# Constants behind the graph's building on ScalarE's queue, x on SyncE's queue, and a fourth buffer for early rows

## The chip, the cores and the metric

The kernel runs on one core of a Trainium2 chip. A core has a matrix engine (TensorE, "PE" in the profile), three engines for other arithmetic (VectorE "DVE", ScalarE "ACT", GpSimd "POOL"), a synchronising engine that mostly starts transfers (SyncE, "SP"), and 16 DMA engines that move data between HBM and the on-chip memory. Any of ScalarE, GpSimd and SyncE can start a transfer from its own queue; a queue is worked off in order. The metric is the device time of one launch in microseconds; smaller is better.

## The reference

One layer of a graph network over 3125 nodes with 256 features. `x` is normalised, sent nine times through the sparse adjacency given by 53,125 weighted edges (the first product is shared by all heads, so that the kernel needs three), mixed by a linear attention, and then sent through a gated network of eight experts.

```python
xn = _layernorm(x, axis=-1)
x = x + _L0_gnn_ref(xn, W0, b0, W1, b1, edge_weight, src, dst) + _L0_mix_ref(xn[None], ...)[0]
x = x + _L0_ffn_ref(_layernorm(x, axis=-1)[None], gate_w, gate_b, w1, b1, w2, b2)[0]

def _L0_gnn_ref(inputs_emb, W0, b0, W1, b1, edge_val, edge_row, edge_col):
    h = _spmm(edge_row, edge_col, edge_val, inputs_emb)
    for _ in range(HEADS):
        outputs = h
        for l, (W, b) in enumerate([(W0, b0), (W1, b1)]):
            z = _spmm(edge_row, edge_col, edge_val, outputs)
            AxW = jax.nn.softmax(z @ W.T + b, axis=1)
            outputs = AxW if l == 0 else jnp.concatenate([AxW, AxW], axis=1)
            ...
```

`dst` is sorted, so the edges of a node lie in one run.

## The kernel before

**Stages.** `from_runs` (L425) first builds a dense adjacency of 3200 x 3200 numbers in HBM (`adj`), from the runs of edges. Then the adjacency, in seven strips of up to 512 columns (`STRIPS`), is multiplied with `xn`, with the result `h` and with the first layer's output: three sweeps over seven strips, each strip 25 rows of 128 x 512. Key/value attention, the gate and the experts are interleaved with and follow these sweeps.

**The building.** It has an order written out by hand (`tc.manual_schedule`), so each engine runs its instructions in the order of the program text.
- `search(c)` (L479) finds, with one matmul (L482) and a few small VectorE operations (L485 to L491), where the runs of 125 groups of five nodes begin. There are five searches; three stand ahead of the first batch and two in the loop, after batches 4 and 6.
- `gather(c)` (L504) issues three indirect transfers on GpSimd's queue: sources, targets, weights (L510). `turn_ends` and `turn_some` bring them into place (transposes L539, ScalarE's copies L542).
- `load_x` (L365) asks for x in two pieces of 12 and 13 tiles of 128 nodes (`X_PIECES`), each behind one of the first two gathers, on GpSimd's queue. The second piece has a tail of 53 rows with a transfer of its own (L113).
- The loop over 40 batches (L698) handles 16 groups at a time: `prepare` makes one-hot operands (VectorE, L615, `selections` L588, `lhs` L624), `widen` casts one of them (ScalarE, L637), `batch` (L643) runs 16 groups of matmuls (L652), copies the sums out in four pieces (ScalarE, L656, `st_rows`), and SyncE writes the batch to `adj` in two transfers (L665 for 112 partitions, L666 for 13).
- As rows of `adj` are finished, `ask` has SyncE load them again (`load_rows`, L668 to L672): tag `a0` for the first strip with four buffers, tag `a1` for the second strip with three. `take` multiplies a loaded row into its strip's sum (L273). In the last batches three `a1` rows are asked for (L733); behind the loop the rest of strip 0 and 15 rows (`AHEAD`) of strip 1 follow. The last row of a strip has 53 nodes.
- `norm_a` to `norm_d` normalise x strip by strip inside the loop.

**The constants.** `make_constants` (L278) reserves memory for the weights of the graph layers, the gate's weights and bias, four normalisation rows and some index tables, in a pool that is open from the start to the end. It returns ten transfers for GpSimd's queue, which are issued behind the third gather (L686), and a generator that forms two gate constants by a matmul with `ones` at batches 22 and 23. `load_w_kv` (L418) is called at batch 24, on GpSimd's queue; w_q, w_o and b_o (L807 to L809) follow behind the building, the gate's rows (in `spread_gate`) much later, all on the same queue.

**Behind the building.** `total` and `found` (L744 to L749) check with one matmul that all edges were met; `found` lies in the pool `build`. Then `ph.close()` gives the building's memory back, and `load_part` (L250) loads blocks of five rows (`at`, L259, with L264 for a strip's 53-row tail) into five buffers in memory that was the building's.

**Semaphores.** The tile framework gives each transfer started by SyncE or ScalarE one of eight completion semaphores, in turn, and lets a transfer wait until the earlier user of its semaphore has landed. GpSimd's transfers have eight of their own.

Of the kernel before, what the change touches and what calls it, by code (L numbers as in the profile page):

```python
# [16 lines left out]
P = 128  # L17
N = 3125
D = 256
# [55 lines left out]
def gps_layer(ctx: ExitStack, tc: tile.TileContext, a: dict, out: bass.AP):  # L75
# [201 lines left out]

    def make_constants():  # L278
        loads = []

        def load(dst, of):
            loads.append(lambda: nc.gpsimd.dma_start(dst, of))

        w0T = const.tile([P, 2, HD], FP)
        load(w0T, a["w0T"].rearrange("(c p) n -> p c n", p=P))
        w1T = const.tile([P, HD], FP)
        load(w1T, a["w1T"])
        b0 = const.tile([P, 1], FP)
        load(b0, a["b0"].rearrange("(p one) -> p one", one=1))
        b1 = const.tile([P, HD], FP)  # L290
        load(b1, rows_all(a["b1"], 0, HD))
# [6 lines left out]
        ones = const.tile([P, P], FP)  # L298
        nc.vector.memset(ones, 1.0)
# [26 lines left out]
        key_base = const.tile([1, NEXP], FP)  # L326
        nc.vector.tensor_copy(key_base, ki)
        held.update(
            w0T=w0T, w1T=w1T, b0=b0, b1=b1, gate_b=gate_b, gate_c=gate_c, gate_m=gate_m, g_lo=g_lo, ones=ones, upto=upto,
            rev=rev, qi=qi, run=run, tok=tok, s_idx=s_idx, key_base=key_base, ln=ln,  # L330
        )

        def finish():

            pm = mm()
            for d in range(2):
                nc.tensor.matmul(
                    pm[:, :NEXP], ones, gate_w[:, d, :], start=(d == 0), stop=(d == 1)
                )
            yield  # L340
            nc.vector.tensor_scalar(gate_m, pm[:, :NEXP], 1.0 / D, None, op0=ALU.mult)
            nc.vector.tensor_tensor(
                gate_c, gate_w, gate_m[:, None, :].to_broadcast([P, 2, NEXP]), ALU.subtract
            )

        return loads, finish()

# [9 lines left out]
    def layer(net, runs):  # L357
# [60 lines left out]
        def load_w_kv():  # L418
            nc.gpsimd.dma_start(w_kv, a["wkv"].rearrange("(c p) n -> p c n", p=P))

# [4 lines left out]
        def from_runs():  # L425
# [13 lines left out]
            for queue, p0, p1, n in (  # L439
# [4 lines left out]
                ))  # L444
            loads, finish = make_constants()
            fi = find.tile([P, 1], I32)
# [32 lines left out]
            def search(c):  # L479
# [6 lines left out]
                    lt, p[:GC, :EK], g_thr[:GC, one],  # L486
                    held["ones"][:GC, 0:1].to_broadcast([GC, EK]), op0=ALU.is_lt,
                    op1=ALU.mult, accum_out=start[:, one],
# [12 lines left out]
            edge_h = build.tile([P, 2, NG + NG % 2], BF)  # L501
            matched = build.tile([GC, NC], FP)

# [52 lines left out]
            fetched = []  # L556
            for c, piece in enumerate(X_PIECES):
                search(c)
                fetched.append(gather(c))
                load_x(nc.gpsimd, *piece)  # L560
            search(2)
            turn_ends(0, *fetched[0])
            turn_some(0, fetched[0][0], edge_h, 1, 2)
# [121 lines left out]
            fetched.append(gather(2))  # L685
            for load in loads:  # L686
                load()

# [9 lines left out]
            for b in range(last + 1):  # L698
# [45 lines left out]
            total = mm()  # L744
            nc.tensor.matmul(total[:1, :NC], held["ones"][:GC, 0:1], matched, start=True, stop=True)
            found = build.tile([1, 1], FP)
            nc.vector.tensor_reduce(found, total[:1, :NC], AX.X, ALU.add)
# [9 lines left out]
        else:  # L757
            general()
            load_w_kv()
            load_x(nc.scalar, 0, NT)  # L760
            for s in range(len(STRIPS)):
# [20 lines left out]
        if runs:  # L782
            to_hT(0, sums[0])


        w0T, w1T, b0, b1, gate_b, gate_c, gate_m, g_lo, ones = (
            held[x]
            for x in ("w0T", "w1T", "b0", "b1", "gate_b", "gate_c", "gate_m", "g_lo", "ones")
        )
# [913 lines left out]
```

## Time and profile before

| | us |
|---|---|
| median of 3 runs | 1017.81 (1017.23 to 1018.5) |
| the profiled execution | 1018.58 |
| its span | 1016.6 |
| TensorE waits in 40 to 290, all releasers | 10.4 |
| the loop's last matmul group starts | 214.37 |
| ScalarE's last copy of `st_rows` starts | 214.79 |
| 60 matmuls on the last 15 rows, start | 224.52 |
| the check of the edge count on TensorE (L745), start | 250.66 |
| first load of an `at` block (L259), issue | 251.39 |

A row of a timeline reads: start, duration, engine, line, operation, output <- inputs, count, and in brackets the idle time ahead of it with what ended it. "PE acc L273 <- DMA a<-adj: 2.6, 2, 1.7" means that matmuls of L273 waited 2.6 us in all, twice, at most 1.7 us, for transfers from `adj` into `a0` or `a1` buffers (the profile leaves the digits out). In the list of transfers "to landing" is the time from the issue to the arrival of the data.

### The profile page before, as it was taken

What the parts mean: (1) busy time and instruction counts of PE and PEld (TensorE: products, weight loads), DVE (VectorE), ACT (ScalarE), POOL (GpSimd) and SP (SyncE); (2) the same over time, 40 slices, a digit from 0 to 9 for tenths busy, and PEclk for the clock granted to TensorE, in tenths of its full rate; (3) what the DMA queues carried; (4) which work ended last, traced back from release to release, by engine and by line L of the source; (5) the groups of instructions that cost most, each with busy time, mean ns of one, the idle gap of its engine ahead of it and who ended that gap; (6) DMA issues with size and microseconds to landing.
All of it is one profiled execution on the core that took longest, in us unless ns stands there. A gap on an engine that the chain in (4) does not pass through costs nothing.

```text
span 1016.6 us, 11457 instructions
## 1 busy us (share of the span) xinstructions
PE 980.6 (96%) x4202; PEld 639.6 (63%) x4202; DVE 514.3 (51%) x1149; ACT 304.6 (30%) x567; POOL 95.6 (9%) x113
## 2 busy tenths in 40 slices
PE   5899999989999999999999999999999989999996
PEld 3878888854444444455765554464544568888985
DVE  7999799800343444445653675584444454221211
ACT  3889889830000001001101001110111214224431
POOL 6411000000000000000000000000111132111111
PEclk9999999999999999999999999999999999999998
DMA  4989888983933247321475657769889896713310
GB/s 144 244 236 260 240 240 238 254 257 108 337 121 103 98 146 205 127 81 47 138 246 194 226 197 269 222 198 376 309 298 298 253 303 226 229 39 124 101 35 20
DMA packets 171641, 197.94 MB, mean 195 GB/s; under 512 B 7664, under 2 KB 118304, under 8 KB 171575
## 3 DMA queue, kind: packets, MB, share of 16 engines
q1 hardware_dynamic: 164285, 178.56, 56.3%
q0 software_dynamic: 7248, 18.51, 6.2%
q8 instruction: 35, 0.57, 0.2%
q14 instruction: 31, 0.25, 0.1%
q10 hardware_dynamic: 42, 0.05, 0.0%
HBM read 144.43 MB, written 53.37 MB: 195 GB/s over the span
## 4 chain that ended last, share of the span: by engine, by line
PE 85%; DMA 4%; DVE 4%; ACT 3%; issue 2%; SPq 1%; POOL 0%; POOLq 0%; ACTq 0%; DVEq 0%
PE acc L273 48%; PE mm L1203 7%; PE acc L1160 7%; PE acc L652 6%; PE b L652 5%; PE mm L831 4%; PE mm L887 2%; DMA at<-adj 2%; PE pk L859 1%; ACT rhs L637 1%; DMA adj<-st_rows 1%; ACT st_rows L656 1%; PE mm L914 1%; PE mm L1011 1%; PE mm L1150 0%
## 5 line engine op out<-in xcount | busy, mean ns | idle before, releaser
L273 PE MATMUL acc<-at,xn 128*128 128x512 f32 (+3 forms) x540 | 203.2, 523 | 1.5 <-DMA at<-adj 1.5
L273 PEld LDWEIGHTS acc<-at,xn 128*128 128x128 f32 (+1 forms) x540 | 96.5, 190 | 89.5 <-issue 75.1
L273 PE MATMUL acc<-at,late 128*128 128x512 f32 (+4 forms) x350 | 139.3, 549 | 3.9 <-DMA at<-adj 3.9
L273 PE MATMUL acc<-at,g 128*128 128x512 f32 (+4 forms) x350 | 137.8, 541 | 0.0
L273 PEld LDWEIGHTS acc<-at,late 128*128 128x128 f32 (+1 forms) x350 | 64.1, 195 | 63.7 <-issue 54.3
L273 PEld LDWEIGHTS acc<-at,g 128*128 128x128 f32 (+1 forms) x350 | 62.9, 190 | 58.6 <-issue 52.3
L652 PE MATMUL acc<-rhs,lhs 128*125 128x128 f32 x626 | 86.4, 282 | 9.0 <-ACT rhs L637 8.1
L652 PEld LDWEIGHTS acc<-rhs,lhs 128*125 128x125 f32 x626 | 78.3, 193 | 20.2 <-ACT rhs L637 9.3
L624 DVE TENSOR_TENSOR lhs<-in_row,in_blk 128x1000 f32<-128x1000 f32 (+1 forms) x79 | 90.3, 1185 | 1.2
L652 PE MATMUL b<-rhs,lhs 128*125 128x128 f32 x624 | 82.9, 277 | 0.0
L652 PEld LDWEIGHTS b<-rhs,lhs 128*125 128x125 f32 x624 | 76.4, 192 | 0.0
L273 PE MATMUL acc<-a,xn 128*128 128x512 f32 (+1 forms) x160 | 72.9, 594 | 2.6 <-DMA a<-adj 2.6
L637 ACT CAST rhs<-cells 128x2048 f32<-128x2048 bf16 x39 | 74.9, 1921 | 0.1
L844 ACT ACTIVATE sq<-kv 128x512 f32<-128x512 f32 x25 | 15.7, 629 | 179.4 <-DVE kv L840 179.4
L1203 PE MATMUL mm<-w,hm 128*128 128x256 f32 (+2 forms) x288 | 64.3, 380 | 0.0
L837 DVE TENSOR_REDUCE kmean<-mm 128x8 f32<-128x512 f32 x25 | 17.3, 691 | 91.6 <-PE mm L831 91.6
L1160 PE MATMUL acc<-xeT,w 128*128 128x208 f32 (+2 forms) x288 | 58.7, 361 | 0.7 <-ACT xeT L1154 0.7
L1203 PEld LDWEIGHTS mm<-w,hm 128*128 128x128 f32 (+2 forms) x288 | 51.2, 180 | 9.6
L1160 PEld LDWEIGHTS acc<-xeT,w 128*128 128x128 f32 x288 | 53.1, 190 | 4.4 <-ACT xeT L1154 0.9
L656 ACT COPY st_rows<-acc 125x512 f32<-125x512 f32 (+1 forms) x79 | 47.7, 603 | 25.2 <-issue 12.4
L1164 ACT ACTIVATE hm<-acc,b_e 128x256 f32<-128x256 f32 (+2 forms) x72 | 32.7, 454 | 65.5 <-PE acc L1160 65.5
L615 DVE TENSOR_TENSOR cells<-steps_w,edge_h 128x2048 bf16<-128x2048 bf16 (+1 forms) x40 | 47.7, 1193 | 4.5 <-ACT rhs L637 4.4
(271 smaller groups left out, 1035.3 us busy)
## 6 DMA issues: line engine op xcount, KB each, us to landing
at<-adj SPq DMA_DIRECT2D x52, 1280.0 KB
adj<-st_rows SPq DMA_DIRECT2D x39, 896.0 KB
at<-adj SPq DMA_DIRECT2D x14, 1024.0 KB
at<-adj SPq DMA_DIRECT2D x12, 960.0 KB
w<-in_f_w SPq DMA_DIRECT2D x10, 1024.0 KB
a<-adj SPq DMA_DIRECT2D x39, 256.0 KB
at<-adj SPq DMA_DIRECT2D x12, 452.5 KB
adj<-st_rows SPq DMA_DIRECT2D x39, 104.0 KB
```

What stands on the lines that cost most here:

```text
L273: nc.tensor.matmul(ps[d][:, :w], stationary(c, d)[:k], a_rows[:k, :w], start=(c == 0), stop=(c == NT - 1),)
L615: nc.vector.tensor_tensor(cells[:, :m, :, :k], steps_w[:, None, :, :k].to_broadcast([P, m, P, k]), of_pairs(1, g0, ng, P), ALU.is_equal,)
L624: nc.vector.tensor_tensor(lhs[:, j::k], in_row[:, j::k, :, None].to_broadcast([P, m, GR, CA]), in_blk[:, :, None, :, j].to_broadcast([P, m ...
L637: nc.scalar.copy(rhs.rearrange("p (i j) c -> p i j c", j=2), cells.rearrange("p i c j -> p i j c"),)
L652: nc.tensor.matmul(p[:GP, j * P : (j + 1) * P], lhs[:, j0 + j], rhs[:, j0 + j], start=True, stop=True,)
L656: nc.scalar.copy(st[:GP, j0 : j0 + nj, :], p[:GP, : nj * P].rearrange("p (g b) -> p g b", b=P),)
L831: nc.tensor.matmul(pkv, xnT[:, d, t * P : (t + 1) * P], w_kv[:, d, :], start=(d == 0), stop=(d == 1),)
L837: nc.vector.tensor_reduce(mean, p3, AX.X, ALU.add)
L887: nc.tensor.matmul(p[:, j * D : (j + 1) * D], xnT[:, d, (t0 + j) * P : (t0 + j + 1) * P], w_mix[:, d, :], start=(d == 0), stop=(d == 1),)
L1160: nc.tensor.matmul(p[:, :slots], w1[:, d, f * P : (f + 1) * P], xeT[:, d, :slots], start=(d == 0), stop=(d == 1),)
L1164: nc.scalar.activation(hm[:, f, :slots], p[:, :slots], AF.Relu, bias=b1_e[:, f : f + 1], scale=1.0)
L1203: nc.tensor.matmul(p[:n, :D], hm[:, f, c : c + n], w2[:, f, :], start=(f == 0), stop=(f == FC - 1),)
```

## The change

- `ones` is made at the start by itself. All other constants, with their index tables, go to a new pool `const_2` that is opened behind the building, in its memory. Their ten loads and that of `w_kv` are issued by ScalarE's queue, kept in the order of the program; w_q, w_o, b_o and the gate's rows are on ScalarE's queue as well. The gate's two constants are formed right there, behind the check of the edge count.
- x is asked for by SyncE's queue behind the third search; a one-element VectorE write into each piece's memory stands ahead of each request.
- Strip 1's early rows have four buffers, and the first of them is asked for one batch earlier, so that four come within the loop.
- `matched` and `found` lie in a pool that outlives the building.

In the built program the ten constant loads stand on ScalarE's queue directly behind its last copy of `st_rows`; on SyncE's queue the loads of strip 1's `at` blocks stand between the last loads of single rows.

```diff
+    ones = const.tile([P, P], FP)
+    nc.vector.memset(ones, 1.0)
+
+    def make_constants(const):
...
         def load(dst, of):
-            loads.append(lambda: nc.gpsimd.dma_start(dst, of))
+            tc.keep_in_program_order(nc.scalar.dma_start(dst, of))
...
-        def finish():
-
-            pm = mm()
-            for d in range(2):
-                nc.tensor.matmul(
-                    pm[:, :NEXP], ones, gate_w[:, d, :], start=(d == 0), stop=(d == 1)
-                )
-            yield
...
-        return loads, finish()
+        pm = mm()
+        for d in range(2):
+            nc.tensor.matmul(pm[:, :NEXP], ones, gate_w[:, d, :], start=(d == 0), stop=(d == 1))
+        nc.vector.tensor_scalar(gate_m, pm[:, :NEXP], 1.0 / D, None, op0=ALU.mult)
+        nc.vector.tensor_tensor(
+            gate_c, gate_w, gate_m[:, None, :].to_broadcast([P, 2, NEXP]), ALU.subtract
+        )
...
         def load_w_kv():
-            nc.gpsimd.dma_start(w_kv, a["wkv"].rearrange("(c p) n -> p c n", p=P))
+            tc.keep_in_program_order(
+                nc.scalar.dma_start(w_kv, a["wkv"].rearrange("(c p) n -> p c n", p=P))
+            )
...
-            loads, finish = make_constants()
...
-            matched = build.tile([GC, NC], FP)
+            matched = keep.tile([GC, NC], FP, tag="matched", name="matched")
...
-            for c, piece in enumerate(X_PIECES):
+            for c in range(2):
                 search(c)
                 fetched.append(gather(c))
-                load_x(nc.gpsimd, *piece)
             search(2)
+            for t0, t1 in X_PIECES:
+
+                nc.vector.memset(xa[:1, t0, :1], 0.0)
+                load_x(nc.sync, t0, t1)
...
-                at = first_a.tile([P, SW], FP, tag=tag, name=tag, bufs=4 if tag == "a0" else 3)
+                at = first_a.tile([P, SW], FP, tag=tag, name=tag, bufs=4)
...
-            for load in loads:
-                load()
...
-                if b in (22, 23):
-                    next(finish, None)
-                if b == 24:
-                    load_w_kv()
...
-                if last - 5 < b <= last - 2:
+                if last - 6 < b <= last - 2:
                     ask(more, ready_1, "a1")
...
-            found = build.tile([1, 1], FP)
+            found = keep.tile([1, 1], FP, tag="sum", name="found")
...
+        make_constants(net.enter_context(tc.tile_pool(name="const_2", bufs=1)))
+        load_w_kv()
...
-        nc.gpsimd.dma_start(w_q, a["wq"].rearrange("(c p) n -> p c n", p=P))
-        nc.gpsimd.dma_start(w_o, a["woT"].rearrange("(c p) n -> p c n", p=P))
-        nc.gpsimd.dma_start(b_o, rows_all(a["bo"], 0, D))
+        nc.scalar.dma_start(w_q, a["wq"].rearrange("(c p) n -> p c n", p=P))
+        nc.scalar.dma_start(w_o, a["woT"].rearrange("(c p) n -> p c n", p=P))
+        nc.scalar.dma_start(b_o, rows_all(a["bo"], 0, D))
...
-            nc.gpsimd.dma_start(raw, rows_all(a["gate_w"], 0, HD * NEXP).rearrange(
+            nc.scalar.dma_start(raw, rows_all(a["gate_w"], 0, HD * NEXP).rearrange(
```

More of the change, by code (lines that the diff above doesn't have):

```diff
@@ L276, in multiply @@
             )
-    def make_constants():
-        loads = []
+    ones = const.tile([P, P], FP)
+    nc.vector.memset(ones, 1.0)
+    def make_constants(const):
         def load(dst, of):
-            loads.append(lambda: nc.gpsimd.dma_start(dst, of))
+            tc.keep_in_program_order(nc.scalar.dma_start(dst, of))
         w0T = const.tile([P, 2, HD], FP)
@@ L295, in make_constants @@
         load(gate_b, rows_all(a["gate_b"], 0, NEXP))
-        ones = const.tile([P, P], FP)
-        nc.vector.memset(ones, 1.0)
         ln = const.tile([P, 4, 64], FP)
@@ L328, in make_constants @@
         held.update(
-            w0T=w0T, w1T=w1T, b0=b0, b1=b1, gate_b=gate_b, gate_c=gate_c, gate_m=gate_m, g_lo=g_lo, ones=ones, upto=upto,
+            w0T=w0T, w1T=w1T, b0=b0, b1=b1, gate_b=gate_b, gate_c=gate_c, gate_m=gate_m, g_lo=g_lo, upto=upto,
             rev=rev, qi=qi, run=run, tok=tok, s_idx=s_idx, key_base=key_base, ln=ln,
         )
-        def finish():
-            pm = mm()
-            for d in range(2):
-                nc.tensor.matmul(
-                    pm[:, :NEXP], ones, gate_w[:, d, :], start=(d == 0), stop=(d == 1)
-                )
-            yield
[L341 to L344, printed above, removed]
-        return loads, finish()
+        pm = mm()
[5 more added lines that the diff above has]
+        )
     y_end = keep.tile([P, 2, D], FP, tag="y_end", name="y_end")
@@ L486, in search @@
                     lt, p[:GC, :EK], g_thr[:GC, one],
-                    held["ones"][:GC, 0:1].to_broadcast([GC, EK]), op0=ALU.is_lt,
+                    ones[:GC, 0:1].to_broadcast([GC, EK]), op0=ALU.is_lt,
                     op1=ALU.mult, accum_out=start[:, one],
@@ L744, in from_runs @@
             total = mm()
-            nc.tensor.matmul(total[:1, :NC], held["ones"][:GC, 0:1], matched, start=True, stop=True)
-            found = build.tile([1, 1], FP)
+            nc.tensor.matmul(total[:1, :NC], ones[:GC, 0:1], matched, start=True, stop=True)
+            found = keep.tile([1, 1], FP, tag="sum", name="found")
             nc.vector.tensor_reduce(found, total[:1, :NC], AX.X, ALU.add)
@@ L758, in layer @@
             general()
-            load_w_kv()
             load_x(nc.scalar, 0, NT)
@@ L783, in layer @@
             to_hT(0, sums[0])
-        w0T, w1T, b0, b1, gate_b, gate_c, gate_m, g_lo, ones = (
+        w0T, w1T, b0, b1, gate_b, gate_c, gate_m, g_lo = (
             held[x]
-            for x in ("w0T", "w1T", "b0", "b1", "gate_b", "gate_c", "gate_m", "g_lo", "ones")
+            for x in ("w0T", "w1T", "b0", "b1", "gate_b", "gate_c", "gate_m", "g_lo")
         )
```

## The prediction

> **What bounds the kernel now.** The page's head comes first: the busy times, and the chain that ended last.
>
> ```profile
> PE 980.6 (96%) x4202; PEld 639.6 (63%) x4202; DVE 514.3 (51%) x1149; ACT 304.6 (30%) x567; POOL 95.6 (9%) x113
> ...
> PE 85%; DMA 4%; DVE 4%; ACT 3%; issue 2%; SPq 1%; POOL 0%; POOLq 0%; ACTq 0%; DVEq 0%
> ```
>
> TensorE is the bound: 36 us of 1016.6 are not its own, so an edit off TensorE gains only where TensorE stands idle, and loses wherever it opens new idle time. Next the stages by windows (columns: stretch and length, then busy time and count of PE, weight loads, DVE, ACT, POOL; granted clock; DMA share; GB/s).
>
> ```profile
> 18.60:43.10 24.50, 21.82 (x164) 20.86 (x164) 23.60 (x37) 18.46 (x25) 13.44 (x16) 1.00 0.97 246
> 43.10:62.50 19.40, 17.12 (x131) 16.24 (x132) 18.15 (x32) 18.67 (x27) 3.81 (x3) 0.91 0.98 272
> 62.50:95.00 32.50, 32.50 (x235) 27.15 (x234) 30.99 (x54) 28.24 (x44) 5.68 (x4) 1.00 0.85 237
> ```
> ```profile
> 214.40:224.50 10.10, 7.49 (x19) 2.96 (x17) 0.00 (x0) 0.27 (x1) 0.00 (x0) 1.00 0.89 250
> 224.50:250.70 26.20, 26.18 (x62) 11.27 (x62) 0.88 (x2) 0.00 (x0) 0.00 (x0) 1.00 0.40 126
> 250.70:265.60 14.90, 13.41 (x47) 6.78 (x47) 5.63 (x12) 1.51 (x3) 2.04 (x3) 1.00 0.88 262
> ```
>
> From 62.5 to 214.4 TensorE has no gap (its windows are full there). The change can act in three places: before 62.5, where VectorE is the busiest (23.60 of 24.50); at the end of the building, 214.4 to 224.5, where TensorE idles 2.6 us; and at 250.7 to 265.6, where it idles 1.5. The waits of TensorE from 40 to 290 us name the releasers:
>
> ```profile
> PE acc L652 <- ACT rhs L637: 5.7, 5, 2.7
> PE acc L273 <- DMA a<-adj: 2.6, 2, 1.7
> PE acc L273 <- DMA at<-adj: 1.5, 2, 1.3
> ```
>
> Last the chain of waits, early and late, with SyncE's queue at the end of the building.
>
> ```profile
> 11.10 3.55 DMA q<-in_edge_weight,start_i
> ...
> 29.91 10.66 DMA adj<-st_rows
> ```
> ```profile
> 214.17 2.11 SPq L672 DMA_DIRECT2D a<-adj  x2
> ...
> 214.79 0.27 ACT L656 COPY st_rows<-acc 125x128 f32<-125x128 f32 x1 [1.35 <-PE acc L652]
> ...
> 220.02 1.07 SPq L672 DMA_DIRECT2D a<-adj  x1
> ...
> 224.52 26.21 PE L273 MATMUL acc<-a,xn 128*128 128x512 f32 x60 [1.68 <-DMA a<-adj]
> ```
>
> A write of adjacency rows took 10.66 us to land, behind x and the constants, and held ScalarE 2.84 us before 40.67. At the end the row asked for at 220.02 landed 4.46 us later, and then 60 matmuls (15 rows of 1.72 us) ran without a gap.
>
> **Part (a), the start.** Removed from the GpSimd queue: x's three DMAs (12.31, 18.51, 19.60; 3.2 MB, the last landing at 28.4) and ten constant loads (25.81 to 33.3). x goes to SyncE's queue as three DMAs at about 10.5, behind the third search's 10.23+0.15 and three tiny memsets on VectorE (the nearest row, a 125x1 operation, took 0.15: at most 0.45 us, all in VectorE's idle 0.84 before 11.22, so nothing; without that cover 0.45). At the windows' 246 to 272 GB/s, 3.2 MB take 12 to 13 us and are in by about 24, ahead of the first write at 25.43. So the 10.66 us landing goes. It isn't worth the 2.84 us of ScalarE or the 2.68 that TensorE lost before 43.10: VectorE has only 0.90 idle to 43.1 and 1.25 to 62.5, mostly waits for the fourth and fifth search on TensorE (0.52 and 0.87). The gain lies between 0 and 2.1; I take 1.2. Against it stands the gather of weights at 11.10, whose landing (3.55) is on the chain into the first cast, `in_row` and `lhs`. It will share the DMA engines with x. Gathers beside SyncE's full writes landed in 4.2 to 6.1 us (41 to 47 and 72 to 76 us): 0.7 to 2.6 later; 0 if x's first bytes come behind it. I take 1.5, since x fills the engines as those writes did. VectorE is in order, so what stands behind `in_row` waits too. Net +0.3, from -2.1 to +2.6.
>
> [...]
>
> **Part (b), the middle.** Two gate matmuls with 8 columns leave the building (0.39 us of TensorE) and come back behind it: 0. A fourth early row of strip 1 moves 256 KB (1.0 us at 251 GB/s) into 185 to 203, where TensorE has no idle time and DMA is at 0.93: 0, hidden by batches prepared ahead; uncovered, 1.0.
>
> **Part (c), the end of the building.** This is where the price is. The order of the built program has all constant loads on ScalarE's queue directly behind its last copy of `st_rows`, which needs the last building matmul. SyncE and ScalarE share eight completion semaphores in turn, and each DMA waits until the earlier user of its semaphore has landed. The counterpart of the first-strip load in the pair of 214.17 now waits for the load of gate_w, the fifth constant. Behind it on SyncE are an a1 load, a full batch's two writes (waiting for gate_b and the first ln row), the counterpart of the load of 220.02, and all later rows.
> - ScalarE's last copy ends at 214.79+0.27 = 215.06. Five issues of 0.35 to 0.62 (small ones on SyncE's queue took 0.30 to 0.47, the only one on ScalarE's 0.62): 1.8 to 3.1. Landing 2.4 (the first table) to 5.0 (the rows of 214.17, used at 219.13): I take 2.3 and 3.0. gate_w in at 220.4 (219.2 to 223.2).
> - Before, 10.3 us went by from 214.17 to the row's landing at 224.47, with older writes in the queue (two issues blocked for 2.11 and 3.12). With the queue drained while SyncE waits, some 3 of these go: 7.0 to 10.3; the middle is 8.6. TensorE resumes at 229.0 (226.2 to 233.5), +4.5.
> - By then it has done one row more than before: 14 rows are left, not 15: -1.72.
>
> Sum +2.8 (0 to +7). What is late next: nothing between 229 and 250, where DMA is at a share of 0.40.
>
> **Part (d), the second strip's loads.** `found` and the constants no longer hold the memory of the next loads: the `at` blocks of strip 1 are asked for between the last rows, not at 251.39 behind the check of the edge count. The 1.5 us of waits go. In exchange four 128-row rows and the 53-row one queue among 256 KB and 1 MB loads. 1 MB is 3.9 us at 267 GB/s, and on top of 4.46 that is 8.4, against five rows or 8.6 us between the freeing of a buffer and its next use: just hidden. The 53-row load asked for at 240.65 trickled at some 25 GB/s until about 247 in the DMA view, 6.4 us; two of them, the `at` tail and the last row, now stand close together, some 12 to 13 us against eight rows or 13.8 us from the buffer's freeing: hidden by one, or late by 3 if SyncE asks 4 us later than it may. Bounds 0 to 3, taken 0.5 as the rows cover it narrowly. Net -1.0 (-1.5 to +1.5). w_q, w_o, b_o and the late gate rows change from GpSimd to ScalarE; TensorE waits for none of them.
>
> [...]
>
> **Sum.** +0.3 + 0 + 2.8 - 1.0 = +2.1 against the profiled execution's own 1018.58 (span 1016.6 and 2.0 around it): 1020.7. That execution lies 0.8 above the median of 1017.81, so on the median's scale 1019.9, say 1020.0. About 0.2% (2.0 us) can be told from no change: slower begins at 1019.8, faster at 1015.8.
>
> **Rivals.**
> 1. *SyncE is hardly held.* gate_w lands by 217.5 (cheap issues, 2.4 landing without backlog): resumption near 225.5, so (c) is +1.0-1.7 = -0.7 and the sum -1.4: 1016.4, with the spread of (a) 1014 to 1018. For it: the loads are small and have a queue of their own. Against: DMA share 0.95 just before.
> 2. *The early stall sets the pace.* If TensorE's 2.68 us before 43.10 come back whole and the weights land as before, (a) is -2.7, not +0.3, and with (c) and (d) as above the sum is -0.9: 1016.9, not slower. It decides from the point where TensorE's gaps end: at 62.5 now, by 60 then. Against: VectorE's 23.60 of 24.50.
> 3. *Both queues bind.* (c) at +5 and the 53-row load 2 late, weights 2.6 late: about +6.5, 1024.3. For it: every lane wait in the row adds up.
>
> Chances: forecast 0.42, rival 1 0.22, rival 2 0.20, rival 3 0.16. The forecast's own range is 1018 to 1022.5; rivals 1 and 2 reach to 1014.5 and rival 3 to 1024.5, so the range is 1014.5 to 1024.5. Slower: 0.7 of the forecast (its costs reach further up than down) and all of rival 3, 0.46. Faster: two thirds of rivals 1 and 2, 0.28. The rest, 0.26.
>
> **What would show it.** (a): the weights' landing above 4.2 us, `in_row` behind 16.3, no stall of ScalarE near 40, TensorE gapless from 61 to 64. (c): a wait of SyncE at the row load for gate_w, its issue at 219 to 223, TensorE resuming at 226 to 233 with 56 matmuls. (d): no wait on `at` after the building, at most a short one on the last rows. If SyncE issues that row before 217, or the gain at 62.5 is over 2 us, the forecast is wrong.

## The result, and the profile after

The changed kernel takes 1031.18 us (1029.33 to 1033.16, 6 runs), beside 1017.69 us for the kernel before on the same chips: a ratio of 1.0128, 95% interval 1.0111 to 1.0145. It is slower, as forecast, but by 13.5 us where the sum had 2.1, and outside the range. The profiled execution took 1030.25 us with a span of 1028.5, 11.9 more than before.

The head of the page, busy times and granted TensorE clock by fortieths of the span:

```profile
PE 984.0 (96%) x4202; PEld 641.1 (62%) x4202; DVE 513.3 (50%) x1151; ACT 304.7 (30%) x567; POOL 83.0 (8%) x95
...
PEclk7999999989899999999999999999999999999999
```

TensorE has the same 4202 matmuls and 3.4 us more busy time. The dips of the clock's row in the ninth and eleventh slice show where part of that comes from; the 7 at the start (half clock from 12.06 to 25.7 us) need not come from the change: e6 below, the kernel before with split loads, has a mean clock of 0.93 in 18 to 43 us too, and e10 and e14, with x on SyncE's queue as here, have 1.00 from 0 to 43. The next view is the windows of the changed kernel around the end of the building (columns as in the prediction).

```profile
216.30:221.50 5.20, 5.17 (x13) 1.95 (x11) 0.00 (x0) 0.27 (x1) 0.00 (x0) 1.00 0.44 103
221.50:229.40 7.90, 0.00 (x0) 0.00 (x0) 0.00 (x0) 0.00 (x0) 0.00 (x0) 0.64 0.50 177
229.40:235.00 5.60, 5.57 (x8) 2.46 (x9) 0.18 (x1) 0.00 (x0) 0.00 (x0) 0.60 1.09 363
...
260.80:264.30 3.50, 3.44 (x6) 1.03 (x6) 0.69 (x1) 0.00 (x0) 0.00 (x0) 0.56 0.67 253
264.30:270.00 5.70, 5.70 (x26) 4.35 (x27) 1.12 (x6) 0.58 (x1) 0.00 (x0) 0.67 0.41 133
```

Where before TensorE idled 2.6 us between 214.4 and 224.5, it now stands still for 8.0, and afterwards it works at a mean clock of 0.60 until 235. The same happens again after 257. TensorE's timeline has the two stalls, and SyncE's list of waits and its timeline have what is behind them:

```profile
216.16 5.32 PE L273 MATMUL acc<-a,xn 128*128 128x512 f32 x12
229.44 28.23 PE L273 MATMUL acc<-a,xn 128*128 128x512 f32 x60 [7.96 <-DMA a<-adj]
260.86 3.44 PE L273 MATMUL acc<-a,xn 53*128 53x512 f32 x4 [3.19 <-DMA a<-adj]
```
```profile
SPq L671 <- DMA gate_w<-in_gate_w: 6.3, 1, 6.3
```
```profile
214.24 0.72 SPq L665 DMA_DIRECT2D adj<-st_rows  x1
221.37 0.82 SPq L671 DMA_DIRECT2D a<-adj  x2
...
249.12 0.24 SPq L671 DMA_DIRECT2D a<-adj  x1
```

SyncE stands 6.3 us at one row load until gate_w is in. The rows are issued at 221.37 and usable at 229.39. Before, 60 matmuls (four for a row) took 26.21 us; now 60 take 28.23, and four more, of the 53-row load, wait 3.19 and take 3.44.

The time from the start to the check of the edge count grew by 13.6 us (250.66 to 264.23). Line by line: the last rows begin 1.57 later (214.59 to 216.16); TensorE resumes another 3.35 later (224.52 to 229.44 in all); one row more, not one fewer, is left then (64 records instead of 60), 1.72; the 60 matmuls take 2.02 longer; the last row comes 3.19 late and takes 1.72 longer. The sum is 13.57.

After that point the lag hardly changes: the last of the 100 matmuls on w0T starts 13.7 us later than before (539.5 against 525.8), the last matmul of the last sweep 14.2 (853.4 against 839.2). The 1.5 us of waits for blocks are gone there, but the clock stays at a half until 268.06, which uses them up. The last stretch of the span, behind the start of the last matmul on `xeT` (the experts' input), is 2.3 us shorter (13.3 against 15.6); why was not tried.

### The profile page after: what moved, and what is told of

Same layout as the page of the kernel before. It is cut to its first block, busy times and chain, and to the rows that moved or that the text cites. A ratio compares the mean times of both kernels' runs of the same rounds, so it can differ in the third digit from the quotient of the medians.

```text
span 1028.5 us, 11463 instructions
## 1 busy us (share of the span) xinstructions
PE 984.0 (96%) x4202; PEld 641.1 (62%) x4202; DVE 513.3 (50%) x1151; ACT 304.7 (30%) x567; POOL 83.0 (8%) x95
## 4 chain that ended last, share of the span: by engine, by line
PE 70%; DMA 9%; issue 7%; DVE 3%; ACT 1%; POOL 1%; SPq 1%; POOLq 0%; ACTq 0%; DVEq 0%
PE acc L273 48%; PE acc L651 5%; PE b L651 5%; DMA out<-y,xe 4%; PE mm L825 4%; PE mm L881 2%; DMA a<-adj 2%; PE pk L853 1%; POOL out L1181 1%; DMA at<-adj 1%; PE mm L908 1%; DMA w_xa<-in_f_w 1%; PE acc L1154 1%; PE mm L1005 1%; DMA xbuf<-rows,s_idx 1%
## 5 line engine op out<-in xcount | busy, mean ns | idle before, releaser
L273 PE MATMUL acc<-a,xn 128*128 128x512 f32 (+1 forms) x160 | 76.4, 619 | 11.2 <-DMA a<-adj 11.2
L273 PEld LDWEIGHTS acc<-a,xn 128*128 128x128 f32 (+1 forms) x160 | 29.7, 197 | 41.9 <-issue 28.5
```

What stands on the lines that cost most here:

```text
L273: nc.tensor.matmul(ps[d][:, :w], stationary(c, d)[:k], a_rows[:k, :w], start=(c == 0), stop=(c == NT - 1),)
```

## The experiments

Fifteen kernels in sixteen runs, each beside the kernel before on its chip. Times are medians; a ratio is to the kernel before, with its 95% interval. The chips differ by some 0.2% and so do the medians of the kernel before (1017.7 to 1019.3).

### Undoing one part at a time

**e1_x_back**: in the changed kernel x is loaded as before.

```diff
-            for c in range(2):
+            for c, piece in enumerate(X_PIECES):
                 search(c)
                 fetched.append(gather(c))
+                load_x(nc.gpsimd, *piece)
             search(2)
-            for t0, t1 in X_PIECES:
-                nc.vector.memset(xa[:1, t0, :1], 0.0)
-                load_x(nc.sync, t0, t1)
```

> The changed kernel with x loaded as before (two pieces on GpSimd's queue, each behind a gather). Theory: x on SyncE's queue makes the first gather's targets and weights land late (first cast of the right operand at 19.15 us instead of 15.46), of which 1.7 us are left at the end of the building; so the first cast comes back to about 15.5, the last building matmul starts near 214.4 instead of 215.9 to 216.1, and the time falls by 1.5 to 2 us, to about 1029.3, with the wait of 8 us at the end of the building unchanged. Rival (the start is repaid by the stall on the third write, 10.66 us to land before): the stall comes back and the time stays within 0.5 us of 1031.2.

1029.53 us, ratio 1.0107 (1.0086 to 1.0127): the size of the theory. The trace tells more. The rows behind the building begin at 212.85, 3.3 us ahead of the changed kernel (216.16) and 1.7 ahead of the kernel before (214.59). These are the two lines, e1's and that of the kernel before:

```profile
212.85 5.32 PE L273 MATMUL acc<-a,xn 128*128 128x512 f32 x12
```
```profile
214.59 3.60 PE L273 MATMUL acc<-a,xn 128*128 128x512 f32 x8
```

And the rival's stall does not come back: x is loaded as before and no write is late near 40 us. So x on SyncE's queue costs 3.3 us in this pair of traces, having the constants elsewhere earns 1.7, and x alone does not make the write land late. Single traces scatter: the rows begin at 216.2 to 217.8 in the six with x on SyncE's queue, at 212.3 to 213.8 in those with x as before, late constants and four buffers, and at 214.6 and 215.6 in the kernel before and e6. That makes the cost 2.4 to 5.5 and the gain 0.8 to 3.3.

**e2_const_pool**: the changed kernel with its late constant loads on GpSimd's queue (w_kv, which nothing holds back there, is loaded at 2.3 us, at the start).

```diff
-            tc.keep_in_program_order(nc.scalar.dma_start(dst, of))
+            nc.gpsimd.dma_start(dst, of)
```

> The changed kernel with all constant loads, w_kv, w_q, w_o, b_o and the gate rows on GpSimd's queue, in the new place in memory. Theory (SyncE's row load waits for the completion semaphore of a constant load of ScalarE, and its data then stand behind ScalarE's small transfers): the row load is issued by 217 instead of 221.4, TensorE's wait of 7.96 us falls below 3 us, the granted clock stays at 1.00 after it, and the time falls by 6 to 9 us, to 1022 to 1025. Rival (the rows are late since strip 1's blocks and a fourth early row load the DMA engines): the wait stays above 6 us and the time at 1029 or more.

1027.06 us, ratio 1.0079 (1.0052 to 1.0107): 4.1 us less by the medians and 5.0 by the ratios, not 6 to 9. The 7.96 us wait is gone; TensorE's longest wait for a row is 3.51, at the 53-row load, where the theory had not looked. A new wait of 2.21 stands for ScalarE's last copy, and that for a write of 209.35 that took 11.09 us to land. The constant loads ran beside it (208.09 to 215.5). The chains of waits have this write in e2, and one like it in the next run, e3, where the constant loads ran from 204 us on:

```profile
209.35 11.09 DMA adj<-st_rows
```
```profile
205.80 10.23 DMA adj<-st_rows
```

**e3_both_back**: both of these edits.

> Both undone at once: x as before, and all constant loads on GpSimd's queue; what is left of the change is the place of the constants behind the building, the four buffers with an earlier first request, and the memory of matched and found. Theory: the sum of the two before, 1019 to 1022; if the early requests for strip 1's blocks are a gain of 1.5 us that outweighs the late 53-row load, as low as 1016.5. Rival (the last row, 53 nodes on one DMA engine, stays late by 3 us and slows the clock): 1021 to 1024.

1023.54 us, ratio 1.0046 (1.0029 to 1.0063), within the rival's span: the last row comes 4.12 us late, and a write of 205.80 took 10.23 to land.

**e4_split**: the changed kernel with 53-row loads cut in two, here and in the blocks.

```diff
-                nc.sync.dma_start(at[:k], adj_rows[c * P : c * P + k, c0 : c0 + SW])
+                for r0, r1 in ((0, P),) if k == P else ((0, 48), (48, LAST)):
+                    nc.sync.dma_start(at[r0:r1], adj_rows[c * P + r0 : c * P + r1, c0 : c0 + SW])
```

> The changed kernel with each 53-row load from the adjacency split into 48 and 5 rows. Theory (a 53-row load runs on one DMA engine, two in a row take 12 us): the wait of 3.19 us ahead of the last row at 260.86 goes, its four matmuls take 1.7 us instead of 3.44 since the clock isn't lowered, and the time falls by 4 to 6 us, to 1025 to 1027. Rival (the last row stands behind the bytes of the three blocks asked for after it and before it): the wait stays above 2 us and the time above 1029.

1021.98 us, ratio 1.0044 (1.0023 to 1.0065): 9.2 us less by the medians and 8.6 by the ratios, more than expected. TensorE's timeline:

```profile
230.78 29.66 PE L275 MATMUL acc<-a,xn 128*128 128x512 f32 x64 [8.71 <-DMA a<-adj]
260.37 0.19 PE L741 MATMUL mm<-matched,ones 125*1 125x5 f32 x2
```

All 16 last rows run in one piece though they begin 1.3 us later. The late row cost 3.9 us up to this check (264.23 to 260.37), and 5.7 by the last sweep's start (698.5 to 692.8) since the clock no longer dips behind it. Another 2.5 come within the last sweep (its last matmul starts at 845.2 against 853.4), and these are not shown to be the split's. A wait of 3 to 4 us for a block stands in that sweep in both traces; in the changed kernel's the clock was at a half for 6.8 us behind it, in e4's it was not. In e5 and e6, which have the split too, the last sweep takes longer (155.4 and 155.5 us) than in the changed kernel (154.9). In the kernel before, only the 53-row load of 240.65 moves data from 243 to 246.5 us: 42 packets of a row each, 25 GB/s, 6.4 and 6.3% of the 16 engines' time, as much as one engine has. How 48 and 5 rows are spread over the engines was not shown; with them the wait of 3.19 us at the last row is gone.

**e5_both_back_split**: e3 with the split. **e6_before_split**: the kernel before with the split.

> x and the constant loads' queue undone, as in the run with both back, and each 53-row load split into 48 and 5 rows. Theory (in that run the last row came 4.1 us late and the clock was then granted at 0.5 to 0.67 for some 10 us): both go, 7 to 9 us, so the time falls from 1023.5 to 1014.5 to 1016.5, below the kernel before. Rival (the split gained 9 us in the changed kernel only since SyncE's queue was late there): it gains 4 us or less here, 1019.5 or more.

> The kernel before with each 53-row load split into 48 and 5 rows, nothing else. Theory (before, the 53-row load of a single row had DMA engines to itself and was in time; only the blocks' tails can gain): between no change and 2.5 us less, 1016 to 1018.4. Rival (the split is worth as much in the kernel before as in the changed one): 1013 or less.

e5: 1017.96 us, ratio 0.9982 (0.9962 to 1.0002), 1.4 us below the 1019.33 of the kernel before there, which the interval does not tell from no change; the gain over e3, by the ratios, is 6.5 us, so the rival falls. e6: ratio 1.0010 (0.9991 to 1.0030), no difference. In the kernel before the 53-row load has slack. The changed kernel, which puts two of them and three blocks close together, pays for it.

**e7_three**: e5 with three a1 buffers, asked for as before.

```diff
-                at = first_a.tile([P, SW], FP, tag=tag, name=tag, bufs=4)
+                at = first_a.tile([P, SW], FP, tag=tag, name=tag, bufs=4 if tag == "a0" else 3)
...
-                if last - 6 < b <= last - 2:
+                if last - 5 < b <= last - 2:
                     ask(more, ready_1, "a1")
```

> As the run with x and the constants' queue undone and the split loads, but with three a1 buffers, first asked for where the kernel before did. Theory (the fourth row is worth its multiplication, 1.7 us, at the end of the building, where TensorE waits, and costs nothing before it): 1 to 2 us slower than with four. Rival (256 KB more in the full stretch of writes delay the last batches as much): the same within 0.7 us, or faster.

1020.21 us, ratio 1.0008 (0.9995 to 1.0020): 2.3 us above e5 on the same chip. The waits for rows are 5.47 us, where e5 has 2.43 and another 1.82 for ScalarE, and the clock in 222 to 229 was 0.51. So in this setting the fourth early row pays, as far as 2.3 us with intervals of 1.3 and 2.0 on either side show it.

### What lowers the clock

**e8_warm**: the changed kernel with idle matmuls ahead of the two late rows.

```diff
+            def idle(n):
+                spare = mm()
+                for _ in range(n):
+                    nc.tensor.matmul(spare, ident, xn[:, 0:2, :], start=True, stop=True)
+
             while ready:
+                s, c, _, _ = ready[0]
+                if (s, c) == (1, 3):
+                    idle(18)
+                if (s, c) == (0, NT - 1):
+                    idle(8)
                 tag = take()
```

> The changed kernel with 26 more matmuls whose result nobody reads: 18 of 128 x 512 ahead of the fourth early row, in place of the wait of 8 us, and 8 ahead of the last row, in place of the wait of 3.2 us. Theory (the clock granted to TensorE falls to 0.5 to 0.67 for some 5 to 10 us after such a wait): the waits are as long as before, but the clock stays at 1.00, the 60 matmuls after the first take 26.2 us instead of 28.2 and the 53-row group 1.7 us instead of 3.4; 4 to 6 us less in all, 1025 to 1027.5. Rival (the matmuls after the waits are slow since DMA writes into their operands' memory, or the clock is lowered for another reason): no gain, or a loss of what the 26 matmuls outlast the waits by, 1031 or more.

1036.33 us, ratio 1.0183 (1.0158 to 1.0208): slower, as the rival has it, but the size of the edit was wrong. One 128 x 512 matmul on these types takes 0.87 us (two records of 0.43), so the 26 took 22.6 us where 10.8 of waits went. The trace still answers the question. These are its windows over the stretches shown above for the changed kernel:

```profile
221.50:229.40 7.90, 7.90 (x20) 3.56 (x19) 0.00 (x0) 0.00 (x0) 0.00 (x0) 1.00 0.36 121
229.40:235.00 5.60, 5.60 (x15) 2.49 (x14) 0.00 (x0) 0.00 (x0) 0.00 (x0) 1.00 1.10 347
```

The clock stays at 1.00, and the 53-row group takes 1.98 us instead of 3.44. With 11.8 us more to do than the waits lasted, the check of the edge count is 8.4 later and the last sweep starts 6.7 later (705.2 against 698.5): 3.4 us came back before the check and 1.7 behind it. Another 1.5 come within the last sweep, where the clock was at a half for 3.4 us in e8's execution and for 6.8 in the changed kernel's; these are not the idle matmuls' doing. The rows were being loaded during the idle matmuls at a DMA share of 0.36 to 1.10, and the clock stayed full, so it is the idleness that lowers it and not the transfers.

In the changed kernel TensorE went idle at 221.48; the granted clock was at 0.50 from 223.69, 2.2 us later, and at 1.00 again from 233.93, 4.5 us after work resumed. The second wait ended at 260.86; there the clock fell only at 261.24, with work already running, and was back at 268.06, 7.2 us after work resumed. Between 26 and 1000 us the traces of this kernel and of the kernel before have five stretches of half clock, of 3.41 us (two), 6.83 (two) and 10.24. How long a wait has to be was not settled: those of 2.09 us (e10) and 2.21 (e2) were followed by half clock (0.76 in 222 to 229 us in both), as were those of 2.43 (e5, 0.76 there) and 2.47 (e9, 0.88 in 235 to 249), while one of 2.08 in the changed kernel, up to 61.18, was not (1.00 to 70), nor was the one of 3.5 in e4's last sweep. So a wait of some 2 us can be enough. After the waits for rows the clock was at a half for 3.4 (e9) to some 10 us (e3: 0.67 in 249 to 260, 0.76 in 260 to 266).

### What holds the rows back

SyncE was released at 221.37 as gate_w landed, but the rows were used only at 229.4. The DMA view of the changed kernel at 222 to 224 us, with packets, megabytes and share by queue:

```profile
DMA packets 250, 0.06 MB, mean 28 GB/s; under 512 B 250, under 2 KB 250, under 8 KB 250
...
q10 hardware_dynamic: 250, 0.06, 11.6%
```

Two row loads and the start of a write had been issued on SyncE's queue (q1), and no packet of theirs moved; ScalarE's (q10) trickled with packets below 512 bytes, at 28 GB/s and 11.6% of the 16 engines' time.

**e9_gated**: e5 with the constants behind a VectorE copy that waits for the end of the adjacency writes. **e10_rows_pool**: e4 with six constants (b1, gate_b, the four of ln: one row spread over 128 partitions each) on GpSimd's queue.

```diff
         nc.vector.memset(hT[:, :, N:], 0.0)
+        held["hT"] = hT
+        make_constants(const_2)
+        load_w_kv()
...
         w0T = const.tile([P, 2, HD], FP)
+        nc.vector.tensor_copy(w0T[:1, 0, :1], held["hT"][:1, 0, N : N + 1])
```

> x as before, the split loads, the four buffers, and the constants in their new place, loaded by GpSimd's queue, but not before a small VectorE copy that stands behind the end of the last adjacency writes; w_kv is loaded there too (in the runs with the constants on GpSimd's queue it went ahead of the gathers, at the start). Theory (in the run without this gate the constant loads ran beside the last full writes from 204 us on, which then landed 10 us late and held ScalarE's last copy): ScalarE's wait of 1.8 us and the lowered clock at 222 to 229 go, TensorE checks the edge count by 249.5 instead of 252.45, and the time falls by 2.5 to 4 us against that run, to 1.5 to 5 us below the kernel before. Rival (the last rows are late by the bytes of strip 1's early blocks): no more than 1 us against that run.

> The changed kernel with the split loads, and with the six constants that are one row spread over 128 partitions (b1, gate_b, the four of ln) loaded by GpSimd's queue; w0T, w1T, b0, gate_w and w_kv stay on ScalarE's. SyncE's row load then waits for w0T, ScalarE's first, instead of gate_w. Theory (two costs in a row: SyncE held by the semaphore, 6.8 us with the split; then its rows, issued at 222.5, move no byte for some 4 us while ScalarE's small transfers trickle): the hold falls to some 3 us, and the rows land within 5.5 us of their issue instead of 7.6; 4 to 6 us less than the split run's 1022. Rival (a row takes 7.6 us to land at this place whatever ScalarE has issued): the landing stays at 7 us or more, and only the shorter hold is gained, 2 to 3 us.

e9: 1019.16 us, ratio 1.0004 (0.9989 to 1.0019); by the ratios 2.2 us more than e5, a difference within the two intervals taken together. ScalarE's wait is gone, and TensorE runs without a gap to 235. Then the rows dry up, in TensorE's timeline:

```profile
212.30 22.82 PE L275 MATMUL acc<-a,xn 128*128 128x512 f32 x52
236.37 1.99 PE L275 MATMUL acc<-a,xn 128*128 128x512 f32 x4 [1.25 <-DMA a<-adj]
239.51 1.98 PE L275 MATMUL acc<-a,xn 128*128 128x512 f32 x4 [1.15 <-DMA a<-adj]
243.96 8.91 PE L275 MATMUL acc<-a,xn 128*128 128x512 f32 x16 [2.47 <-DMA a<-adj]
```

The blocks of the next strips, asked for between the rows from 222.67 on, stand in their way: DMA share 0.92 to 1.05 from 229 to 249, where the kernel before had 0.25 to 0.67. The check comes at 252.80, as late as in e5.

e10: 1020.56 us, ratio 1.0017 (1.0003 to 1.0031). By the ratios that is 2.7 us less than e4. This doesn't decide: the hold moved to a write of SyncE's (6.0 us behind an older write), since GpSimd's small loads now ran beside the last writes, as in e2; the rows still landed 7.4 us after their issue.

**e13_before_no_rows** and **e14_split_no_rows** leave the six loads out, in the kernel before and in e4.

```diff
-        load(b1, rows_all(a["b1"], 0, HD))
+        nc.vector.memset(b1, 0.1)
...
-        load(gate_b, rows_all(a["gate_b"], 0, NEXP))
+        nc.vector.memset(gate_b, 0.0)
...
-        for i, name in enumerate(("ln_k_g", "ln_v_g", "ln_k_b", "ln_v_b")):
-            load(ln[:, i, :], rows_all(a[name], 0, 64))
+        nc.vector.memset(ln, 1.0)
```

> The kernel before without the loads of b1, gate_b and the four rows of ln (fixed values are written into their memory instead). Theory (these six loads hold up SyncE's transfers): the write issued near 29.9 lands in 6 us or less instead of 10.66, ScalarE's wait of 2.8 us near 40 and TensorE's 2.7 us before 43 are gone, though x is loaded as before; the time falls by 0 to 1.5 us, since VectorE is the bound there. Rival (x fills the DMA engines): the landing stays at 9 us or more and the waits stay.

> The changed kernel with the split loads and without the loads of b1, gate_b and the four rows of ln (fixed values are written instead); w0T, w1T, b0, gate_w and w_kv stay on ScalarE's queue. SyncE is then held at most for w0T. Theory (the six loads hold up SyncE's transfers): the single rows at the end of the building land within 5 us of their issue instead of 7.6 to 8.7, TensorE waits less than 3 us there instead of 8.7, and the time falls from 1022 by 5 us or more, to 1017 or less. Rival (the place, w_kv or the writes make them late): the landing stays at 7 us or more, TensorE waits 4 us or more, and the time stays at 1019 or more.

Their total times (3300.61 and 3307.45 us) can't be compared: with other values in these six the program goes on far beyond the usual end, to a span of 3296 and more. Up to 300 us the instructions are the same, and that part is read. In e13 ScalarE has no wait for a write up to 62 us, with x as before; SyncE's queue writes on without the block of 5.68 us at 34.51 that the kernel before has. First the line of the kernel before, then e13's:

```profile
34.51 5.68 SPq L666 DMA_DIRECT2D adj<-st_rows  x1
```
```profile
29.00 3.18 SPq L665 DMA_DIRECT2D adj<-st_rows  x1
32.22 1.45 SPq L664 DMA_DIRECT2D adj<-st_rows  x1
33.72 2.61 SPq L665 DMA_DIRECT2D adj<-st_rows  x1
```

Its rows behind the building begin at 213.49, 1.1 us earlier than in the kernel before. In e14, at the end of the building:

```profile
217.81 5.32 PE L275 MATMUL acc<-a,xn 128*128 128x512 f32 x12
223.90 3.70 PE L275 MATMUL acc<-a,xn 128*128 128x512 f32 x8 [0.78 <-DMA a<-adj]
228.96 24.80 PE L275 MATMUL acc<-a,xn 128*128 128x512 f32 x56 [1.35 <-DMA a<-adj]
```

2.1 us of waits instead of 8.7, the check of the edge count at 253.68 instead of 260.37, with w0T, w1T, b0, gate_w and w_kv loaded by ScalarE at the same place. So the six loads are what held SyncE's transfers up, in both places; x and w_kv are cleared. What in the six does it was not tried apart. In e14 SyncE was also held for less (1.5 us for w0T, 0.8 for w1T and 1.4 for b0), so the 6.7 us are hold and trickle together. The harm has bounds: in e12 and e15 below, the same six loads run from GpSimd's queue at 227 to 231 us, beside single rows, and TensorE waits for none of these rows (busy for 6.00 us of the 6.00 from 229 to 235).

### A version that beats both

**e11_x_later**: e9 with x in three pieces, the last two at batches 6 and 11.

> As the gated run, with x on GpSimd's queue in three pieces: 8 tiles behind the first gather, 8 at batch 6, 9 at batch 11, each ahead of the batch that normalises it. Theory (before 62 us VectorE is the bound, with 0.9 us idle to 43 and 1.25 to 62, so the late write landing at 40 us costs little): 0.5 to 1.5 us less than the gated run. Rival (TensorE's 2.7 us before 43 come back whole): 2.5 us less or more.

1018.58 us, ratio 1.0000 (0.9988 to 1.0012), 0.6 below e9 on that chip: the theory's size, but within the noise of both. VectorE, busy for 23.60 of 24.50 us there in the kernel before, leaves little to gain.

**e12_late_blocks**: e9 with the first five blocks held back until the edge count is checked; run twice. **e15_landed**: held back only until the last single row is in.

```diff
         at = pool.tile([P, CH, SW], FP, tag="at", name="at")
+        if held.get("landed") is not None and held.setdefault("blocks", 0) < 5:
+            held["blocks"] += 1
+            nc.vector.tensor_copy(at[:1, :, 0], held["landed"].to_broadcast([1, CH]))
...
+            held["landed"] = keep.tile([1, 1], FP, tag="landed", name="landed")
+            nc.vector.tensor_copy(held["landed"], last_row[0][:1, :1])
             total = mm()
```

> As the gated run, with the first five blocks of the strips behind the building held back by small VectorE copies until the edge count is checked, as in the kernel before. Theory (the blocks asked for early take the DMA engines from the last single rows, which cost 4.9 us of waits, more than the 1.5 us they save): TensorE multiplies the last rows without waits and checks the edge count by 246 instead of 252.8; the first blocks then come 1 to 2 us late; 3 to 5 us less than the gated run, and less than the kernel before by as much. Rival (the last rows are late for another reason, such as two loads in flight only): waits for single rows stay above 3 us and the time within 1.5 us of the gated run's.

> The run with the blocks held back once more, on whatever chip comes. Theory: 1 to 4 us below the kernel before, ratio 0.996 to 0.999. Rival (the first result was chance): a ratio of 0.9995 or more.

> As the run with the blocks held back, but only until the last single row has landed, near 240 us, instead of the check of the edge count at 248 to 249. Theory (DMA is idle from the last row's landing to the check): the 2.0 us for which TensorE waited for the first blocks go and nothing else moves, 1 to 2 us less than the run held back to the check. Rival (the blocks' memory is that of rows still being multiplied, so they come no earlier): the same within 0.7 us.

e12: 1016.51 and 1015.59 us, ratios 0.9980 (0.9966 to 0.9994) and 0.9968 (0.9954 to 0.9982), by the ratios 2.4 and 3.7 us below e9. Its rows no longer dry up:

```profile
222.92 24.80 PE L278 MATMUL acc<-a,xn 128*128 128x512 f32 x56 [0.42 <-DMA a<-adj]
```

The check is at 247.65, 5.2 ahead of e9, and 2.0 are lost again to the first blocks. e15: 1012.58 us, ratio 0.9931 (0.9910 to 0.9951), less than the kernel before by 6.1 us by the medians and 7.0 by the ratio. Its rows and blocks:

```profile
212.98 8.75 PE L278 MATMUL acc<-a,xn 128*128 128x512 f32 x20
223.30 24.50 PE L278 MATMUL acc<-a,xn 128*128 128x512 f32 x56 [1.57 <-DMA a<-adj]
...
248.31 1.10 PE L278 MATMUL acc<-at,xn 128*128 128x512 f32 x2
```

One gap of 1.57 us, none for a block (asked for at 241.72), the clock at 1.00 from 222 to 272 us. Against e12's second run, on the same chip, e15 is 3.0 us faster; 2.0 of these are the waits for the first blocks. In its profiled execution the last sweep was shorter too (151.8 us, against 154.0 and 155.4 in e12's two), and the page's clock row has a 9 throughout it, where e12's first has an 8; whether that is more than chance was not tried. It has the constants behind the building, four buffers, the split loads, x as before, and each transfer asked for when the one that matters more is out of its way.

## Why the prediction was wrong, and where it was right

**Direction and place**: right, though the forecast lay only 0.2 us above what can be told from no change. The price lies at the end of the building, at SyncE's row load, and part (b) cost nothing that shows.

**(a), +0.3 predicted, +1.57 measured**: mis-sized on both sides, and the cause of the gain was wrong. The first gather's transfers were slowed more than the rows beside full writes showed: targets, issued at 9.61, were in at 15.38 (5.8 us; before 3.4), and weights, issued at 11.14, at about 18.3 (7.2; before 3.55), where the bound was 6.1. The cost was 3.3, bounds 0 to 2.6. The gain was 1.7 (e1), near the 1.2, but it came without moving x: in e13 the early write lands in time with x as before and the six loads left out. Both sizes are of one pair of traces, with the scatter given at e1. The reading that TensorE has no gap from 62.5 to 214.4 was not quite right either: it waits 1.4 us there; no term rests on it.

**(c), the hold**: right. gate_w was foreseen in at 220.4 (219.2 to 223.2), and SyncE was released at 221.37, with the building 1.6 later. TensorE's resumption was foreseen at 229.0 and came at 229.44. In part that is luck: from the issue at 221.37 to 229.39 it took 8.0 us, near the 8.6 of the sum, but the sum put them down to older writes in the queue. Measured were some 4 us in which no packet of SyncE's queue moved and ScalarE's small loads trickled, and without the six loads a row was used 4.8 us after its issue (e14).

**(c), the count of rows**: this step failed. "By then it has done one row more than before: 14 rows are left, not 15" gives the fourth buffer's row as done. But the fourth a1 row is asked for behind the held load, and so late with it. Three rows were done and 16 left: 1.72 lost instead of 1.72 gained, 3.4 us of the error. That could have been read from the order of SyncE's queue, on which this part of the prediction itself is built.

**(c), "What is late next: nothing"**: this step failed too, and is the larger part. After the wait of 8 us the clock is halved for 4.5 us of work: the 60 matmuls take 2.0 us longer. After the second wait the 53-row group takes 1.7 us longer, and some 1.8 more are lost behind the check (e4 against the changed kernel). No term of the sum had it. From 214 to 265 us the kernel before keeps a clock of 1.00, with waits of at most 1.7. But the prediction's own row for 43.10 to 62.50 shows 0.91: in that trace the wait of 2.68 us before 43.10 is followed by half clock from 44.55 to 47.96.

**(d), -1.0 predicted**: the 1.5 us of waits for blocks went as foreseen, but the 53-row load was taken at 0.5 where it cost 3.19, just outside the bounds of 0 to 3. Issued at 249.12, it was in at 260.81, 11.7 us later. The narrow cover was named ("hidden by one, or late by 3"), and the value taken was the optimistic one. With the clock behind it, it cost 5.7 us by the start of the last sweep (e4). The 12 to 13 us for two such loads were an estimate, twice the 6.4 of one, and no run shows how far two overlap; from the issue of the `at` tail at 246.77 to the arrival of the last row it took 14.0. And the early blocks are no gain: they take the last rows' place in the DMA engines (e9 against e12: share 0.92 in 235 to 249 us against 0.32, the check at 252.80 against 247.65).

**Rivals**: the third, "Both queues bind", was the right one in kind; its 1024.3 lacked the row count and the clock. The first is out, since SyncE was held for 6.3 us. The second asks for weights that land as before, and they landed 3.7 us later. In e1, where the gathers are as before and the stall is gone, the gain is 1.7 and not the 2.7; with a scatter of 0.8 to 3.3 that speaks against it and does not exclude it.

## What to carry to other kernels

A stall of a saturated TensorE is priced twice: the wait itself, and, behind most waits over 2 us in these traces, half a clock for the next 3 to 10 us; look at the granted clock behind every wait over some 2 us. When loads are moved to another queue, list for each shared completion semaphore which load now waits for which, and count everything behind the held one, before crediting a deeper buffer. Loads that spread one short row over all partitions, and loads like the 53-row one here (25 GB/s, 6.4% of the 16 engines' time), belong where nothing else is due: the first did their harm beside writes of 896 KB (10.2 to 11.1 us to land), and on ScalarE's queue ahead of SyncE's rows (some 4 us without a packet).

## What the hardware showed that was not expected

- Six loads of 4 to 64 KB, each one row spread over 128 partitions, kept megabytes of other transfers waiting: a write of 896 KB took 10.2 to 11.1 us to land beside them (e2, e3, and 10.66 in the kernel before), and rows issued behind them moved no packet for some 4 us, at a DMA share of 0.12 from 222 to 224 us. Without the six, in the same places, neither happened (e13, e14). On GpSimd's queue beside single rows of 256 KB they held up nothing that TensorE waited for (e12, e15: busy for 6.00 of 6.00 us from 229 to 235).
- The granted clock fell to 0.50 2.2 us into the wait of 7.96 us, and 0.4 us after the end of the wait of 3.19; waits of 2.09 and 2.21 us were enough too (e10, e2). The five stretches of half clock between 26 and 1000 us, in this kernel's trace and that of the kernel before, last 3.41, 6.83 or 10.24 us.
- Cutting a 53-row load into 48 and 5 rows was worth 8.6 us (by the ratios) in the changed kernel, up to 2.5 of them perhaps the clock of the last sweep, and nothing measurable in the kernel before.
